# Separate buffers for the filter loop, two of chunk 0's matrix banks made earlier, and the filter banks read back in four steps

## Chip, cores and metric

The kernel runs on one core of a Trainium2 chip. The metric is the device time of one execution in microseconds (us), given as the median of several runs. Everything is float32. PE is the matrix engine, DVE the vector engine, ACT the scalar engine, POOL the GpSimd engine; SP is the engine that issues nearly all DMA transfers.

## The reference

The input is x of shape 8 x 1024 tokens x 128 channels (8 images of 32 x 32). Layer 0 adds an attention block to it. Layer 1 first adds a two-directional state-space block to the tokens t, and then adds a spectral filter of the layer-normed tokens. Only that last step matters here:

```
un  = layer_norm(t)                                  # per token
out = sum over k of  irfft(rfft(phi_k) * rfft(un)) @ (s_k * M_phi_plus[k])     # 16 filters
    + the same with un * (+1,-1,+1,...)  and M_phi_minus                       # signs undone after
    + un[t] @ M_u[0] + un[t-1] @ M_u[1] + un[t-2] @ M_u[2]                     # three-tap products
t   = t + out * (selected bank)                      # one of four filter banks, by log_weights + gumbel
```

The selected bank has 2 x 16 matrices of 128 x 128. For each of 128 frequencies the filters turn them into one matrix per frequency (a weighted sum over the 16 filters), and the spectra of the tokens are multiplied with it.

## The kernel before

All eight images stay on the chip through the first part, as tiles X[0] to X[7] of 128 partitions x 8 x 128. Then come three stages that matter here.

**End of the unit stage** (lines 1448 to 1545). The last two of 16 state-space units are finished while the layer norm, the spectra and the three-tap products of images 0 and 1 are already made. All engines, SP too, run in program order here. Near the end line 1541 adds the last unit's rows to X[7] and stores it to `xd`; line 1542 (`reload(u)`) reads it back in another order of tokens; line 1544 adds the three-tap products to X[1], and `store_residual(1)` (line 1545) writes X[1] to `xa`.

**Spectra stage** (lines 1558 to 1625, pools f_...). For images b = 2 to 7, `transform(b)` transposes the normed tokens on PE (cpt, line 561), multiplies them with the Fourier table (pf, line 571), combines the parts on ACT, DVE and POOL into sp, and stores sp (1 MB) to `ud`. One turn later `taps_of(b, k)` makes the three-tap products of two halves k (pu, line 601), adds them to X[b] on DVE (line 611), and `store_residual(b)` writes X[b] (512 KB) to `xa`. In between `turned(n, ...)` handles a quarter n of the selected bank's matrices: it loads 8 of them (`md`, 512 KB), transposes them on PE (mdt), copies them on DVE and stores them to `me` in DRAM. After the fourth quarter, four transfers read all of `me` back into `mst`, so that its partition is the filter number (32 of them) times the group g of four. PE, DVE, ACT and POOL run in program order; the order of SP is left to the scheduler.

**Filter loop** (lines 1629 to 1744, pools g_...). There are 16 chunks of 8 frequencies. `matrices(c, n, gs)` makes an eighth n of chunk c's frequency matrices: 16 products of mst and taps on PE (pg), into four PSUM banks, and four copies to gs, alternately by ACT and DVE. `loaded_spectra(c)` loads the chunk's spectra u from `ud` and makes their turned copy on POOL. `apply` multiplies them with gs (py). The loop runs one chunk ahead: chunk c + 1's matrices stand between the four applies of chunk c, and chunk 0's eight banks stand alone in front. gs (64 KB per partition) and u (8 KB) have two buffers each in pool g_2. These lie where the X tiles lay (`middle.close()`, lines 1626 and 1627, gives that space back), so the first gs waits for the last X to be stored. Then a last stage fetches the filtered spectra back (early_yt, room), transforms them (pz) and writes the output.

The lines that order the spectra stage, before:

```
for b in range(2, B + 1):
    ...
    if b > 2:
        taps_of(b - 1, 0)
    if 2 <= b <= 5:
        turned(b - 2, *((ps_o, "o", 4) if b == 2 else (ps_t, "t", 8)))
    if b > 2:
        taps_of(b - 1, 1)
        store_residual(b - 1)
```

The whole functions, with the profile's line numbers:

Of the kernel before, what the change touches and what calls it, by code (L numbers as in the profile page):

```python
# [10 lines left out]
ALU = mybir.AluOpType  # L11
# [34 lines left out]
def fast_kernel(ctx: ExitStack, tc: tile.TileContext, a: dict, out: bass.AP, bad: bass.AP):  # L46
# [883 lines left out]
    with ExitStack() as s:  # L930
# [608 lines left out]
        scale_rows(u)  # L1539
        third = shift_of(3, resid, *norms.pop(3), "_next")  # L1540
        add_rows(u)
        reload(u)
        for k in range(NB):
            add_taps(1, k, po[:, k])
        store_residual(1)
# [7 lines left out]
    with ExitStack() as s:  # L1553
        mp = s.enter_context(tc.tile_pool(name="c_m", bufs=1, side="right"))
        mst = mp.tile([P, 32, C], F32, tag="mst", name="mst")
        early_yt = mp.tile([P, 2, 4, 4, C], F32, name="early_yt")

        with ExitStack() as s2:
            p1 = s2.enter_context(tc.tile_pool(name="f_1", bufs=1))
            p2 = s2.enter_context(tc.tile_pool(name="f_2", bufs=2))  # L1560
            ps_f = s2.enter_context(tc.tile_pool(name="f_ps_f", bufs=2, space=PSUM))
            ps_o = s2.enter_context(tc.tile_pool(name="f_ps_o", bufs=2, space=PSUM))
            ps_t = s2.enter_context(tc.tile_pool(name="f_ps_t", bufs=1, space=PSUM))

            def turned(n, pool, tag, size):

                t = p2.tile([P, 8, C], F32, tag="md", name=f"md{n}")
                nc.sync.dma_start(t, md.rearrange("d r k e -> d (r k) e")[:, n * 8 : n * 8 + 8, :])
                to = p2.tile([P, 8, C], F32, tag="me", name=f"me{n}")
                for at in range(0, 8, size):  # L1570
                    pt = pool.tile([P, size, C], F32, tag=tag, name=f"mdt{n}_{at}")
                    for i in range(size):
                        nc.tensor.transpose(pt[:, i, :], t[:, at + i, :], ident)  # L1573
                    nc.vector.tensor_copy(
                        to[:, at : at + size].rearrange("p k d -> p (k d)"), pt.rearrange("p k d -> p (k d)")
                    )
                nc.sync.dma_start(me[:, n * 8 : n * 8 + 8, :], to)
                if n == 3:
                    for g in range(4):
                        nc.sync.dma_start(  # L1580
                            mst[g * 32 : (g + 1) * 32],
                            me[g * 32 : (g + 1) * 32].rearrange("n k d -> k n d"),
                        )

            def transform(b):

                un = xns.pop(b).rearrange("p (k r) c -> p k r c", k=NB)
                pt = ps_t.tile([P, NB, 4, P], F32, tag="t", name=f"cpt{b}")
                turn_spectra(un, pt)
                uts[b] = p2.tile([P, 4, NB * P + 1], F32, tag="ut", name=f"ut{b}")  # L1590
                nc.gpsimd.memset(uts[b][:, :, 0:1], 0.0)
                sp = p2.tile([P, NF // FC, NB, 2, 4, FC], F32, tag="sp", name=f"sp{b}")
                for k in range(NB):
                    pf = ps_f.tile([P, 4, 2, NF], F32, tag="f", name=f"pf{b}_{k}")
                    sd = p2.tile([P, 2, 2, 2, NF], F32, tag="sd", name=f"sd{b}_{k}")
                    later = p2.tile([P, 2, 2, NF], F32, tag="later", name=f"later{b}_{k}")
                    for _ in block_spectra(k, un, pf, sd, later, sp):
                        pass
                store_spectra(b, sp)
                copy_turned(uts[b], pt)  # L1600

            def taps_of(b, k):
                po = ps_o.tile([P, 4, C], F32, tag="o", name=f"pu{b}_{k}")
                regress(b, k, uts[b], po)
                add_taps(b, k, po)

            s2.enter_context(tc.manual_schedule(engines=IN_ORDER))
            uts = {}
            for _ in scaled(3, *third, p2):
                pass  # L1610
            for b in range(2, B + 1):
                if b + 2 < B:
                    norms[b + 2] = normalize(p2, b + 2)
                if b < B:
                    transform(b)
                if 3 < b + 1 < B:
                    for _ in normalized(b + 1, p2, *norms.pop(b + 1), wide=p2):
                        pass
                if b > 2:
                    taps_of(b - 1, 0)  # L1620
                if 2 <= b <= 5:
                    turned(b - 2, *((ps_o, "o", 4) if b == 2 else (ps_t, "t", 8)))
                if b > 2:
                    taps_of(b - 1, 1)
                    store_residual(b - 1)
        middle.close()
        middle.close()

        with ExitStack() as s2:
            p2 = s2.enter_context(tc.tile_pool(name="g_2", bufs=2))  # L1630
            p3 = s2.enter_context(tc.tile_pool(name="g_3", bufs=3))
            ps_g = s2.enter_context(tc.tile_pool(name="g_ps_g", bufs=8, space=PSUM))

            turn = 0

            def matrices(c, n, gs):

                nonlocal turn
                pts = [ps_g.tile([P, 4, P], F32, tag="g", name=f"pg{c}_{n}_{g}") for g in range(4)]
                cols = slice(c * FC, (c + 1) * FC)  # L1640
                for e in range(4):
                    for g in range(4):
                        rows = slice(g * 32, (g + 1) * 32)
                        nc.tensor.matmul(  # L1644
                            pts[g][:, e, :],
                            lhsT=mst[rows, n * 4 + e, :],
                            rhs=taps[rows, cols].rearrange("p f q m i -> p (f q m i)"),
                            start=True,
                            stop=True,
                        )  # L1650
                for g, pt in enumerate(pts):
                    to = gs[:, :, n * 16 + g * 4 : n * 16 + g * 4 + 4]
                    frm = pt.rearrange("p e n -> p n e")
                    if turn % 2:
                        nc.vector.tensor_copy(to, frm)  # L1655
                    else:
                        nc.scalar.copy(to, frm)  # L1657
                    turn += 1

            def loaded_spectra(c):  # L1660

                u = p2.tile([P, 2, NB, B, 2, 4 * FC], F32, tag="u", name=f"u{c}")
                for k in range(NB):
                    nc.sync.dma_start(
                        u[:, 0, k].rearrange("p b i f -> p b (i f)"), ud[c][:, :, k].rearrange("p b i q f -> p b (i q f)")
                    )
                nc.gpsimd.tensor_scalar(u[:, 1, :, :, 0, :], u[:, 0, :, :, 1, :], -1.0, None, ALU.mult)  # L1667
                nc.gpsimd.tensor_copy(u[:, 1, :, :, 1, :], u[:, 0, :, :, 0, :])
                return u

            def apply(c, n, q, gs, u, py):

# [42 lines left out]
                )  # L1715

            chunks = NF // FC
            gs, us, gathered = {}, {}, {}
            s2.enter_context(tc.manual_schedule(engines=IN_ORDER))
            for c in range(-1, chunks):  # L1720
                if c + 1 < chunks:
                    gs[c + 1] = p2.tile([P, P, C], F32, tag="gs", name=f"gs{c + 1}")
                    us[c + 1] = loaded_spectra(c + 1)
                else:

                    room = p2.tile([P, P, C], F32, tag="gs", name="room")
                    res = [room[:, :32, :], mp.tile([P, 32, C], F32, tag="mst", name="res1")]
                    res = [t.rearrange("p (b r) c -> p b r c", b=B) for t in res]
                    load_residuals(1, 0, B)
                    load_residuals(0, 0, 4)  # L1730

                for n in range(4):
                    if c + 1 < chunks:
                        matrices(c + 1, 2 * n, gs[c + 1])
                        matrices(c + 1, 2 * n + 1, gs[c + 1])
                    if c >= 0:
                        half, turn = divmod(n, 2)
                        py = ps_g.tile([P, 2, C], F32, tag="g", name=f"py{c}_{n}")
# [15 lines left out]
                if n == 2:  # L1754
                    load_residuals(0, 4, 4)
            for yt, (k, h) in zip(yts, pieces):
                z = p2.tile([P, 2, 2, 4, C], F32, tag="u", name=f"z{k}_{h}")
                for r, i, op in ((0, 0, ALU.subtract), (0, 1, ALU.add), (1, 0, ALU.add), (1, 1, ALU.subtract)):
                    nc.vector.tensor_tensor(z[:, r, i], yt[:, i, :, 2, :], yt[:, 1 - i, :, 3, :], op)
                blk = NB - 1 - k  # L1760
# [830 lines left out]
```

## Time and profile before

| what | value |
|---|---|
| median of 3 runs | 1403.44 us (1398.19 to 1407.6) |
| the profiled execution's own time | 1403.45 us |
| its span, first to last instruction | 1401.6 us |
| mean granted PE clock | 0.98 |
| busy share of the span | PE 95%, DVE 79%, ACT 66%, POOL 38% |

Busy times by stage, from windows of the trace (us):

| stretch | length | PE | DVE | ACT | POOL | PE clock | DMA share |
|---|---|---|---|---|---|---|---|
| 999 to 1010, image 2 and the first quarter of the bank | 11.0 | 5.7 | 5.4 | 4.0 | 7.9 | 0.87 | 0.96 |
| 1010 to 1022.4, image 3 | 12.4 | 12.4 | 7.4 | 5.3 | 8.0 | 0.84 | 0.65 |
| 1022.4 to 1033, image 4 | 10.6 | 10.6 | 7.8 | 5.3 | 7.4 | 1.00 | 0.76 |
| 1057.5 to 1069.2, last three-tap products | 11.7 | 10.9 | 4.8 | 1.6 | 6.1 | 1.00 | 1.18 |
| 1069.2 to 1076.4 | 7.2 | 2.1 | 0.5 | 0.6 | 0.0 | 0.93 | 0.61 |
| 1076.4 to 1088.4, chunk 0's matrices | 12.0 | 12.0 | 10.6 | 9.0 | 4.1 | 0.76 | 0.48 |
| 1105 to 1340, filter loop | 235.0 | 229.1 | 171.8 | 128.0 | 28.8 | 1.00 | 0.28 |

All times in this text are microseconds from the start of the span unless something else is said. A line of the profile names the source line, the engine and the tile that is written and those that are read (`gs<-pg`: the copy from PSUM tile pg to gs). A float32 product on PE shows as two records. A DMA issue on SP is shown with the time that issuing it took, not with the time of the transfer. The chain of waits is followed back from the last instruction: at each step to what released it. "Granted clock" is PE's clock as a share of full speed.

### The profile page before, as it was taken

Reading aid. Unit: us, or ns where it says so; the run is one execution under the profiler, and the core shown is the slowest. Engines: PE = TensorE matmul, PEld = TensorE weight load, DVE = VectorE, ACT = ScalarE, POOL = GpSimd, SP = SyncE. Lnnn points to the kernel's source line nnn. Section 1 sums busy time; section 2 is a strip of 40 time slices with the busy share of each in tenths; the row PEclk is TensorE's granted clock in tenths of the full one; section 3 lists DMA queues with packets and bytes.
Section 4 is the critical chain, followed back from the end, with each engine's and each line's share of the span. In section 5 each row is a group of like instructions: output and inputs, shape, how many; then the busy total and the mean of one; then the engine's idle time right before and its main releaser. Section 6 shows DMA issues by size and latency. Waiting matters only on the chain. (4 is left out here: it accounts for less than half of the span.)

```text
span 1401.6 us, 47569 instructions
## 1 busy us (share of the span) xinstructions
PE 1330.1 (95%) x20926; PEld 844.7 (60%) x20926; DVE 1103.4 (79%) x2145; ACT 922.8 (66%) x1428; POOL 536.0 (38%) x510
## 2 busy tenths in 40 slices
PE   7999999999999999999999999998898999999967
PEld 4333333333333666666666666667797988888964
DVE  5789888788778688988889898999564777777745
ACT  5666666766756888888878888876353555555520
POOL 3412986876910343434343343444673011111100
PEclk9999999999999999999999999999999999999979
DMA  7100111111101434444444343431668132222357
GB/s 172 55 2 2 38 39 39 53 39 39 31 1 42 96 78 93 108 94 113 94 108 94 92 95 88 114 83 48 197 208 198 46 78 73 77 69 70 83 171 294
DMA packets 139391, 123.24 MB, mean 88 GB/s; under 512 B 44808, under 2 KB 118152, under 8 KB 135080
## 3 DMA queue, kind: packets, MB, share of 16 engines
q1 hardware_dynamic: 137048, 115.93, 32.0%
q8 instruction: 166, 2.72, 0.8%
q10 hardware_dynamic: 2128, 4.19, 0.8%
q14 instruction: 49, 0.40, 0.1%
HBM read 78.15 MB, written 34.08 MB: 80 GB/s over the span
## 5 line engine op out<-in xcount | busy, mean ns | idle before, releaser
L809 ACT ACTIVATE pr<-pt 128x1024 f32<-128x1024 f32 x256 | 248.2, 1022 | 105.0 <-PE pt L804 103.9
L1657 ACT COPY gs<-pg 128x512 f32<-128x512 f32 x256 | 133.1, 603 | 75.6 <-PE pg L1644 58.4
L1655 DVE COPY gs<-pg 128x512 f32<-128x512 f32 x256 | 159.1, 685 | 26.0 <-PE pg L1644 18.9
L834 DVE TENSOR_TENSOR two<-pr,pr 128x1024 f32<-128x1024 f32 x128 | 164.8, 1328 | 15.2 <-ACT pr L809 15.2
L804 PE MATMUL pt<-q,k 32*128 32x512 f32 x1024 | 162.5, 651 | 6.1 <-ACT pr L809 4.1
L1644 PE MATMUL pg<-taps,mst 32*128 32x128 f32 x4096 | 150.1, 283 | 11.9 <-issue 5.8
L1644 PEld LDWEIGHTS pg<-taps,mst 32*128 32x128 f32 x4096 | 135.0, 189 | 27.2 <-issue 19.3
L825 PE MATMUL po<-pr,v 128*32 128x512 f32 x1024 | 140.6, 610 | 0.0
L1678 PE MATMUL py<-gs,u 128*32 128x128 f32 (+1 forms) x4096 | 130.9, 281 | 3.4 <-issue 3.4
L1030 POOL TENSOR_TENSOR ec<-ec,ct 128x2048 f32<-128x2048 f32 x16 | 83.6, 5224 | 112.3 <-ACT ct L1110 57.1
L1072 DVE SCALAR_TENSOR_TENSOR xs<-xp,cw,xs 128x1024 f32<-128x1024 f32 x96 | 122.5, 1283 | 2.2 <-issue 0.2
L1678 PEld LDWEIGHTS py<-gs,u 128*32 128x32 f32 (+1 forms) x4096 | 114.8, 141 | 10.9 <-issue 3.6
L1094 PE MATMUL pb<-bxt,wbc 128*128 128x512 f32 x256 | 114.0, 597 | 3.6 <-ACT zs L1085 3.6
L1667 POOL TENSOR_SCALAR u<-u 128x512 f32<-128x512 f32 x16 | 24.0, 1499 | 237.5 <-DMA u<-ud 138.3
L804 PEld LDWEIGHTS pt<-q,k 32*128 32x128 f32 x1024 | 49.5, 185 | 88.9 <-ACT pr L809 27.1
L1193 DVE SCALAR_TENSOR_TENSOR state<-state,dec,pst 128x64 f32<-128x64 f32 x448 | 87.3, 275 | 1.1
L1302 POOL TENSOR_TENSOR rms<-rms_v,mhalf 128x8 f32<-128x8 f32 x16 | 26.5, 1659 | 157.0 <-DVE rms_v L1300 157.0
L1094 PEld LDWEIGHTS pb<-bxt,wbc 128*128 128x128 f32 x256 | 47.1, 189 | 60.3 <-issue 55.0
L825 PEld LDWEIGHTS po<-pr,v 128*32 128x32 f32 x1024 | 27.8, 110 | 89.7 <-issue 86.4
L1016 POOL TENSOR_TENSOR lm<-cs,lm 128x2048 f32<-128x2048 f32 x16 | 57.9, 3620 | 57.7 <-DVE xs L1072 22.6
L845 PE MATMUL pd<-two,ones 128*32 128x512 f32 x512 | 74.1, 618 | 2.3 <-DVE two L834 2.1
L1272 PEld LDWEIGHTS spo<-wo,y 128*128 128x128 f32 x512 | 62.1, 191 | 13.1 <-issue 8.9
(310 smaller groups left out, 2784.5 us busy)
## 6 DMA issues: line engine op xcount, KB each, us to landing
lm<-cd SPq DMA_DIRECT2D x32, 512.0 KB
ec<-cd SPq DMA_DIRECT2D x32, 512.0 KB
ud<-sp SPq DMA_DIRECT2D x8, 1024.0 KB
u<-ud SPq DMA_DIRECT2D x32, 256.0 KB
yd<-sums SPq DMA_DIRECT2D x32, 256.0 KB
moved<-state SPq DMA_DIRECT2D x48, 128.0 KB
room<-yd SPq DMA_DIRECT2D x6, 1024.0 KB
X<-in_x SPq DMA_DIRECT2D x8, 512.0 KB
```

The costliest lines, as they stand in the source:

```text
L804: nc.tensor.matmul(pt[:, i, :], lhsT=k[rows, j * P : (j + 1) * P], rhs=q[rows, cols], start=True, stop=True)
L809: nc.scalar.activation(pr[:, 2 * g : 2 * g + 2, :].rearrange("p i t -> p (i t)"), pt.rearrange("p i t -> p (i t)"), AF.Exp, scale=SCALE,)
L825: nc.tensor.matmul(po[rows, :], lhsT=vs[b][:, j, rows], rhs=pr[:, h, :], start=(j == 0), stop=(j == NT - 1))
L834: nc.vector.tensor_tensor(two, sums["pr"][:, 2 * g : 2 * g + 2, :], pr[:, 2 * g : 2 * g + 2, :], ALU.add)
L1030: t = nc.gpsimd.tensor_tensor(u.ec, u.ec, u.ct.unsqueeze(1).to_broadcast([P, NH, NT, L]), ALU.mult)
L1072: u.convolved = nc.vector.scalar_tensor_tensor(acc, xp[:, at : at + T], cw[u.d][:, n, i : i + 1], acc, ALU.mult, ALU.add)
L1094: nc.tensor.matmul(u.pb[:, i * 512 : (i + 1) * 512], lhsT=wbc[u.d][:, k, :], rhs=xt[:, at : at + 512], start=(k == 0), stop=(k == KC - 1),)
L1193: nc.vector.scalar_tensor_tensor(u.state[:, k, h, :], u.state[:, k - 1, h, :], u.dec[:, c, h, j : j + 1], u.pst[c][:, j, h, :], ALU.mult, ...
L1644: nc.tensor.matmul(pts[g][:, e, :], lhsT=mst[rows, n * 4 + e, :], rhs=taps[rows, cols].rearrange("p f q m i -> p (f q m i)"), start=True, ...
L1655: nc.vector.tensor_copy(to, frm)
L1657: nc.scalar.copy(to, frm)
L1678: nc.tensor.matmul(py[t * 32 : t * 32 + 32 - 16 * m, q // 2, :], lhsT=u[:, i, m:, :, :, q * FC + f].rearrange("p k b i -> p (k b i)"), rhs ...
```

## The change

Three things are done.

1. **Buffers.** gs and u no longer rotate in one pool with two buffers. Even chunks take `first_gs`, a pool on the other side of the memory that is opened before the spectra stage and does not overlap X; odd chunks take `second_gs`, opened in the filter loop where X lay. early_yt moves to a pool of its own, opened in the filter loop. `room` and the z tiles of the last stage take the same two pools in turn.
2. **Two banks earlier.** `matrices` gets its PSUM tiles from its caller. `double_banks` makes a bank of chunk 0 in the spectra stage, with two of that stage's pf tiles. `planned` puts one after the first half of image 7's three-tap products and one after the second half. Chunk 0's spectra are loaded at the end of the spectra stage.
3. **Banks one by one.** Three quarters of the bank are loaded up front, the fourth when the first has been transposed. `turned(0)` to `turned(3)` stand at b = 3 to 6 instead of 2 to 5, all with the same PSUM tile. `spread(n)` reads quarter n back into mst at the beginning of turn b = n + 4, with four transfers of 8 partitions each (128 KB) in place of four of 32 partitions each (512 KB) at the end. The spectra stage now runs SP in program order too, and `reload` of X[7] stands there, behind the first bank load.

```diff
-        reload(u)
         for k in range(NB):
             add_taps(1, k, po[:, k])
         store_residual(1)
...
-        early_yt = mp.tile([P, 2, 4, 4, C], F32, name="early_yt")
+        first_gs = s.enter_context(tc.tile_pool(name="c_g", bufs=1, side="right"))
+
+        def chunk_matrices(c, pool):
+            return pool.tile([P, P, C], F32, tag="gs", name=f"gs{c}")
...
+            def load_bank(n):
+                mds[n] = pm.tile([P, 8, C], F32, tag="md", name=f"md{n}")
+                nc.sync.dma_start(mds[n], md.rearrange("d r k e -> d (r k) e")[:, n * 8 : n * 8 + 8, :])
+
+            def turned(n):
+
+                if n == 0:
+                    load_bank(3)
+                pt = ps_t.tile([P, 8, C], F32, tag="t", name=f"mdt{n}")
+                for i in range(8):
+                    nc.tensor.transpose(pt[:, i, :], mds[n][:, i, :], ident)
                 to = p2.tile([P, 8, C], F32, tag="me", name=f"me{n}")
...
+                nc.vector.tensor_copy(to.rearrange("p k d -> p (k d)"), pt.rearrange("p k d -> p (k d)"))
+                nc.sync.dma_start(me[:, n * 8 : n * 8 + 8, :], to)
+
+            def spread(n):
+                for g in range(4):
+                    nc.sync.dma_start(
+                        mst[g * 32 + n * 8 : g * 32 + n * 8 + 8],
+                        me[g * 32 : (g + 1) * 32, n * 8 : n * 8 + 8].rearrange("n k d -> k n d"),
                     )
-                nc.sync.dma_start(me[:, n * 8 : n * 8 + 8, :], to)
-                if n == 3:
-                    for g in range(4):
-                        nc.sync.dma_start(
-                            mst[g * 32 : (g + 1) * 32],
-                            me[g * 32 : (g + 1) * 32].rearrange("n k d -> k n d"),
-                        )
...
-            s2.enter_context(tc.manual_schedule(engines=IN_ORDER))
-            uts = {}
-            for _ in scaled(3, *third, p2):
+            s2.enter_context(tc.manual_schedule(engines=ALL_IN_ORDER))
+            uts, mds = {}, {}
+            for n in range(3):
+                load_bank(n)
+                if n == 0:
+                    reload(units[-1])
+            gs, begun = {0: chunk_matrices(0, first_gs)}, set()
+
+            def double_banks(n):
+                pts = [ps_f.tile([P, 2, 4, P], F32, tag="f", name=f"pg0_{n}_{i}") for i in range(2)]
+                begun.add((-1, n))
+                matrices(0, n, gs[0], [pts[g // 2][:, g % 2] for g in range(4)])
+
+            def ahead(b, place):
+                for _ in range(planned.get((b, place), 0)):
+                    double_banks(len(begun))
+
+            planned = {(B, 1): 1, (B, 2): 1}
+            for _ in scaled(3, *third, px):
                 pass
             for b in range(2, B + 1):
+                if 4 <= b <= 7:
+                    spread(b - 4)
...
+                ahead(b, 0)
                 if b > 2:
                     taps_of(b - 1, 0)
-                if 2 <= b <= 5:
-                    turned(b - 2, *((ps_o, "o", 4) if b == 2 else (ps_t, "t", 8)))
+                ahead(b, 1)
+                if 3 <= b <= 6:
+                    turned(b - 3)
                 if b > 2:
                     taps_of(b - 1, 1)
                     store_residual(b - 1)
+                ahead(b, 2)
+            us = {0: loaded_spectra(0, first_gs)}
...
+            second_gs = s2.enter_context(tc.tile_pool(name="g_g", bufs=1))
+            yp = s2.enter_context(tc.tile_pool(name="g_y", bufs=1, side="right"))
+            early_yt = yp.tile([P, 2, 4, 4, C], F32, name="early_yt")
...
                 if c + 1 < chunks:
-                    gs[c + 1] = p2.tile([P, P, C], F32, tag="gs", name=f"gs{c + 1}")
-                    us[c + 1] = loaded_spectra(c + 1)
+                    if c >= 0:
+                        gs[c + 1] = chunk_matrices(c + 1, second_gs if c % 2 == 0 else first_gs)
+                        us[c + 1] = loaded_spectra(c + 1, second_gs if c % 2 == 0 else first_gs)
...
-                        matrices(c + 1, 2 * n, gs[c + 1])
-                        matrices(c + 1, 2 * n + 1, gs[c + 1])
+                        for i in range(2 * n, 2 * n + 2):
+                            if (c, i) not in begun:
+                                matrices(c + 1, i, gs[c + 1], single_banks(c + 1, i))
...
-                z = p2.tile([P, 2, 2, 4, C], F32, tag="u", name=f"z{k}_{h}")
+                z = (second_gs if h else first_gs).tile([P, 2, 2, 4, C], F32, tag="u", name=f"z{k}_{h}")
```

More of the change, by code (lines that the diff above doesn't have):

```diff
@@ L1555, in fast_kernel, with loaded_spectra, matrices @@
         mst = mp.tile([P, 32, C], F32, tag="mst", name="mst")
-        early_yt = mp.tile([P, 2, 4, 4, C], F32, name="early_yt")
+        first_gs = s.enter_context(tc.tile_pool(name="c_g", bufs=1, side="right"))
+        def chunk_matrices(c, pool):
+            return pool.tile([P, P, C], F32, tag="gs", name=f"gs{c}")
+        def loaded_spectra(c, pool):
+            u = pool.tile([P, 2, NB, B, 2, 4 * FC], F32, tag="u", name=f"u{c}")
+            for k in range(NB):
+                nc.sync.dma_start(
+                    u[:, 0, k].rearrange("p b i f -> p b (i f)"), ud[c][:, :, k].rearrange("p b i q f -> p b (i q f)")
+                )
+            nc.gpsimd.tensor_scalar(u[:, 1, :, :, 0, :], u[:, 0, :, :, 1, :], -1.0, None, ALU.mult)
+            nc.gpsimd.tensor_copy(u[:, 1, :, :, 1, :], u[:, 0, :, :, 0, :])
+            return u
+        turn = 0
+        def matrices(c, n, gs, pts):
+            nonlocal turn
+            cols = slice(c * FC, (c + 1) * FC)
+            for e in range(4):
+                for g in range(4):
+                    rows = slice(g * 32, (g + 1) * 32)
+                    nc.tensor.matmul(
+                        pts[g][:, e, :],
+                        lhsT=mst[rows, n * 4 + e, :],
+                        rhs=taps[rows, cols].rearrange("p f q m i -> p (f q m i)"),
+                        start=True,
+                        stop=True,
+                    )
+            for g, pt in enumerate(pts):
+                to = gs[:, :, n * 16 + g * 4 : n * 16 + g * 4 + 4]
+                frm = pt.rearrange("p e n -> p n e")
+                if turn % 2:
+                    nc.vector.tensor_copy(to, frm)
+                else:
+                    nc.scalar.copy(to, frm)
+                turn += 1
         with ExitStack() as s2:
-            p1 = s2.enter_context(tc.tile_pool(name="f_1", bufs=1))
+            px = s2.enter_context(tc.tile_pool(name="f_x", bufs=2))
             p2 = s2.enter_context(tc.tile_pool(name="f_2", bufs=2))
+            pm = s2.enter_context(tc.tile_pool(name="f_m", bufs=3))
             ps_f = s2.enter_context(tc.tile_pool(name="f_ps_f", bufs=2, space=PSUM))
@@ L1563, in fast_kernel @@
             ps_t = s2.enter_context(tc.tile_pool(name="f_ps_t", bufs=1, space=PSUM))
-            def turned(n, pool, tag, size):
-                t = p2.tile([P, 8, C], F32, tag="md", name=f"md{n}")
-                nc.sync.dma_start(t, md.rearrange("d r k e -> d (r k) e")[:, n * 8 : n * 8 + 8, :])
-                to = p2.tile([P, 8, C], F32, tag="me", name=f"me{n}")
[L1570 to L1575, printed above, removed]
-                    )
-                nc.sync.dma_start(me[:, n * 8 : n * 8 + 8, :], to)
-                if n == 3:
-                    for g in range(4):
-                        nc.sync.dma_start(
-                            mst[g * 32 : (g + 1) * 32],
-                            me[g * 32 : (g + 1) * 32].rearrange("n k d -> k n d"),
-                        )
+            def load_bank(n):
[7 more added lines that the diff above has]
+                    nc.tensor.transpose(pt[:, i, :], mds[n][:, i, :], ident)
+                to = p2.tile([P, 8, C], F32, tag="me", name=f"me{n}")
+                nc.vector.tensor_copy(to.rearrange("p k d -> p (k d)"), pt.rearrange("p k d -> p (k d)"))
+                nc.sync.dma_start(me[:, n * 8 : n * 8 + 8, :], to)
+            def spread(n):
+                for g in range(4):
+                    nc.sync.dma_start(
+                        mst[g * 32 + n * 8 : g * 32 + n * 8 + 8],
+                        me[g * 32 : (g + 1) * 32, n * 8 : n * 8 + 8].rearrange("n k d -> k n d"),
+                    )
             def transform(b):
@@ L1616, in fast_kernel @@
                 if 3 < b + 1 < B:
-                    for _ in normalized(b + 1, p2, *norms.pop(b + 1), wide=p2):
+                    for _ in normalized(b + 1, p2, *norms.pop(b + 1), wide=px):
                         pass
+                ahead(b, 0)
                 if b > 2:
                     taps_of(b - 1, 0)
-                if 2 <= b <= 5:
-                    turned(b - 2, *((ps_o, "o", 4) if b == 2 else (ps_t, "t", 8)))
+                ahead(b, 1)
+                if 3 <= b <= 6:
+                    turned(b - 3)
                 if b > 2:
@@ L1631, in fast_kernel, with single_banks @@
             p3 = s2.enter_context(tc.tile_pool(name="g_3", bufs=3))
+            second_gs = s2.enter_context(tc.tile_pool(name="g_g", bufs=1))
+            yp = s2.enter_context(tc.tile_pool(name="g_y", bufs=1, side="right"))
+            early_yt = yp.tile([P, 2, 4, 4, C], F32, name="early_yt")
             ps_g = s2.enter_context(tc.tile_pool(name="g_ps_g", bufs=8, space=PSUM))
[L1634 to L1669, printed above, removed]
+            def single_banks(c, n):
+                return [ps_g.tile([P, 4, P], F32, tag="g", name=f"pg{c}_{n}_{g}") for g in range(4)]
             def apply(c, n, q, gs, u, py):
@@ L1717, in fast_kernel @@
             chunks = NF // FC
-            gs, us, gathered = {}, {}, {}
+            gathered = {}
             s2.enter_context(tc.manual_schedule(engines=IN_ORDER))
@@ L1721, in fast_kernel @@
                 if c + 1 < chunks:
-                    gs[c + 1] = p2.tile([P, P, C], F32, tag="gs", name=f"gs{c + 1}")
-                    us[c + 1] = loaded_spectra(c + 1)
+                    if c >= 0:
+                        gs[c + 1] = chunk_matrices(c + 1, second_gs if c % 2 == 0 else first_gs)
+                        us[c + 1] = loaded_spectra(c + 1, second_gs if c % 2 == 0 else first_gs)
                 else:
-                    room = p2.tile([P, P, C], F32, tag="gs", name="room")
+                    room = chunk_matrices(c + 1, first_gs)
                     res = [room[:, :32, :], mp.tile([P, 32, C], F32, tag="mst", name="res1")]
```

## The prediction

> **What bounds the kernel now.** I read the page first (PE busy 95% of the span), then the chain of waits through the two stages that the change touches, then SP's and DVE's orders of time there, then windows for the DMA rates. The profiled execution took 1403.45 us of device time with a span of 1401.6; the median of the runs shown is 1403.44, so a difference in the span is taken over to the median as it is. One run in three strayed by 5 us.
>
> The chain of waits (start, us, what):
>
> ```profile
> 999.19 1.75 PE pf L571 x8
> 1000.95 6.92 DMA md<-md
> 1008.00 1.94 PE mdt L1573 x8
> 1009.94 1.71 PE cpt L561 x8
> 1011.65 4.65 PE pf L571 x16
> ...
> 1057.66 10.73 PE pu L601 x96
> 1068.42 0.76 DVE X L611
> ...
> 1069.60 5.75 DMA xa<-X
> ...
> 1076.45 12.06 PE pg L1644 x250
> ```
>
> PE carries the chain except for two holes. In the first, PE waits 5.11 us for a bank (md<-md), and then works slowly: mdt 1.94 for what later takes 0.87, cpt 1.71 for 0.87, pf 4.65 for 3.46. In the second, chunk 0's first copies wait until the last residual store has left X, because gs lies where X lay; PE idles 5.16 us, and the prologue then lasts to the first apply at 1088.43. From there PE is full to 1346, and nothing in the change touches that loop's work.
>
> DVE ends the prologue: 12 of its copies of 128x512 follow each other without a gap, 0.61 each, beside PE's 1.05 per bank (2.1 for two):
>
> ```profile
> 1082.42 7.27 DVE L1655 COPY gs<-pg 128x512 f32<-128x512 f32 x12 [0.42 <-PE pg L1644]
> ```
>
> SP's order of time near the read-back of the banks, and DMA windows (last two columns: mean busy share of the DMA engines, GB/s; the column before them is PE's clock):
>
> ```profile
> 1044.13 0.37 SPq L592 DMA_DIRECT2D ud<-sp  x1
> 1044.61 1.81 SPq L1577 DMA_DIRECT2D me<-me  x1
> 1046.85 0.85 SPq L614 DMA_DIRECT2D xa<-X  x1
> 1050.90 4.57 SPq L1580 DMA_DIRECT2D mst<-me  x4
> 1058.40 6.37 SPq L614 DMA_DIRECT2D xa<-X  x1
> ```
>
> ```profile
> 661.00:669.00 8.00, 8.00 (x57) 5.37 (x57) 6.51 (x7) 5.83 (x7) 0.00 (x0) 1.00 1.03 216
> 1008.00:1009.00 1.00, 1.00 (x5) 1.00 (x6) 0.00 (x0) 0.00 (x0) 1.00 (x3) 0.50 1.00 287
> 1048.50:1051.00 2.50, 2.50 (x25) 2.50 (x24) 1.67 (x4) 1.95 (x6) 2.50 (x7) 1.00 1.04 398
> 1054.00:1063.00 9.00, 9.00 (x68) 8.59 (x67) 3.45 (x6) 2.15 (x4) 5.53 (x11) 1.00 1.23 180
> ```
>
> Stores from 128 partitions (me, xa) run at 398 GB/s. The loads lm and ec, into 64 partitions each, run at 216 with the engines full. The read-back mst<-me, into 32 partitions per transfer, runs at 180. Its 2 MB held the rings from 1052 to 1063[...].
>
> [...] The fetches into early_yt (8 partitions) write 8 completions each in the trace. [...]
>
> **The change part by part.**
>
> First hole: turned(0) goes from b=2 to b=3, and banks 0 to 2 are asked for ahead. On SP, in program order now, md0 follows xa(1) at about 1001.3 and lands near 1009; PE wants it at 1011.6. PE passes from pf (ends 1002.88) to cpt3, which waits only for ACT's copies of cpt2 (end 1004.49). A hole of 1.7 us should leave the clock up. cpt3 0.87 + pf 3.46 from 1004.55 gives 1008.9 instead of 1016.29: **-7.4**. mdt3 now falls into b=6, +0.87; pu(7,0) ends at 1059.2.
>
> Banks ahead: two of the eight banks (1.05 each on PE) stand around pu(7,1). Their four ACT copies fall in ACT's idle 16.49 us; of the four on DVE two fit DVE's gap of 1.93 between add_taps, and two start the prologue. Nothing is added on PE, only moved.
>
> Buffers apart: gs0 no longer waits for xa. If the banks were there in time: pu(7,0) 1059.2 + 1.05 + pu(7,1) 2.68 + 1.05 + 0.1 + 16 DVE copies at 0.615 (18 before, two done) 9.84 = first apply at 1073.9 against 1088.43, **-14.5**. u0 would come 6 us after xa(7), and POOL's 1.51 + 0.60 fit. Chunk 1's copies now wait for xa(7), some 10 us after it was issued: covered. early_yt's new place, the z tiles' pools and the reload issued behind md0 cost nothing: the fetches begin at 1108, z keeps its rotation, X7 is wanted at b=5, over 10 us later. If that cover were gone, each would cost its landing, about 6.
>
> Read-back one by one: four transfers of 512 KB become sixteen of 128 KB, 12 more issues on SP (four took 4.57). Each goes to 8 partitions. Four follow one another per bank set[...]. Call T the time that they hold those rings. [...] From below: the fetch at 1177.9 moved its 128 KB by 1179.4, 85 GB/s, so 6.2; [...]a 512 B packet at the 27 ns of the ud store, 128 per engine, 3.5. The fetch is short[...] (169 GB/s at first, 26 at its end), so I take T = **9.5**.
>
> SP is in order here. Per b it holds: read-back of the bank before (waits for that me to land), ud (1 MB), me, xa. From ud's issue to me landed is 6.77 (1044.13 to 1050.90), so one turn takes 6.75 + T, against PE's 10.56 (0.87 + 3.46 + 2.68 + 0.87 + 2.68). With T = 9.5 it is 16.3: the rings fall behind by 5.7 a turn. The first read-back starts about 1027.3 (ud3 waits for POOL until 1017.5; + 6.77 + 1.6 for md3 + 1.05 issue and rounding 0.4). The fourth has landed at 1027.3 + 3 x 6.75 + 4T + 1 = 1048.6 + 4T = **1086.6**. Every bank's matmuls read all 128 partitions of mst, so pg0 stands until then from 1059.2, and behind it in PE's order pu(7,1), behind that add_taps, xa(7) and u0. After 27 us PE is at half clock for about 6 us: pg0 2.1, pu(7,1) 4.65, pg1 1.05, then 0.1 + 9.84: 17.7. First apply at 1104.3 against 1088.43: **+15.9**. sp6 and sp7 would wait up to 6 us for late ud stores, beside PE. Sum: 1403.4 + 15.9 = 1419.3.
>
> **The rivals.**
> Read-back harmless (the other side): the four small transfers hide beside the products. One mechanism decides, T, in the 8-partition read-back: 1066.3 + 4T = 1088.4 gives T = 5.5. Below it the change wins: T = 3.5 lands at 1062.6 and gives 1066.3 + 4 x 3.5 = 1080.3, -8, 1395; from T = 2.6 down the whole -14.5 stays, 1389. For it: the fetch's first 64 KB ran at full packet speed (84 ns for 2 KB). Against: its last packets took 300 ns and more[...].
> A draw: T between 5 and 6, the front's gain paid back by the stall, 1401 to 1406. For it stands the 85 GB/s[...].
> The change doing less than it says: if SP still put the bank loads late, PE would keep the first hole; the rest stays as above, and with T = 9.5 the rings' start moves little: 1419 to 1426.
>
> **How the numbers follow.** A change of 1%, 14 us, is about what a measurement of this kernel can tell from none. Read-back bound, with the late-load case: 0.78; T from 6.2 to 11.7 gives +2.7 to +24.7, own range 1406 to 1428. Harmless: 0.17, 1389 to 1399. Draw: 0.05. Slower by over 1% needs T above 9.0, about two thirds of the first case: 0.52. Faster by over 1% needs nearly the whole -14.5: 0.06. Within 1%: 0.42. The range leaves out the best of the harmless case and the worst of the first: 1395 to 1428.
>
> **What would show it.** Right: PE goes from pf to cpt3 without a bank wait, clock 1.00 at 1008; the four mst<-me of each b lie 16 us apart on SP; PE's longest wait is pg on mst, over 20 us; 0.50 after it. Wrong: the last mst<-me issued before 1056 and pg0 near 1060; or DMA rates over 100 GB/s in those stretches.

## The result, and the profile after

Measured side by side, the kernel before took 1401.54 us (median of 6 runs) and the changed one 1415.72 (6 runs, 1409.88 to 1422.45): ratio 1.0104, interval 1.0066 to 1.0143. The change made the kernel about 1% slower. The profiled execution of the changed kernel took 1414.91 us, with a span of 1413.2.

The chain of waits of this execution names only its last two steps, so PE's order of time is read instead (start, busy time, what; in brackets the idle time before it and what ended it):

```profile
1004.73 1.09 PE L561 MATMUL cpt<-ident,ln_x 128*128 128x128 f32 x8 [1.66 <-ACT ut L566]
1005.65 3.62 PE L571 MATMUL pf<-fwd,ln_x 128*128 128x256 f32 x16
...
1051.35 8.20 PE L601 MATMUL pu<-m_u,ut 128*128 128x128 f32 x72
1078.64 0.79 PE L1580 MATMUL pg<-taps,mst 32*128 32x128 f32 x2 [19.09 <-DMA mst<-me]
1081.30 0.79 PE L1580 MATMUL pg<-taps,mst 32*128 32x128 f32 x2 [1.87 <-DMA mst<-me]
1083.83 0.79 PE L1580 MATMUL pg<-taps,mst 32*128 32x128 f32 x2 [1.74 <-DMA mst<-me]
1086.03 2.07 PE L1580 MATMUL pg<-taps,mst 32*128 32x128 f32 x26 [1.41 <-DMA mst<-me]
1088.03 3.63 PE L601 MATMUL pu<-m_u,ut 128*128 128x128 f32 x24
1091.59 1.17 PE L1580 MATMUL pg<-taps,mst 32*128 32x128 f32 x32
1094.76 9.71 PE L1580 MATMUL pg<-taps,mst 32*128 32x128 f32 x256 [1.99 <-DVE gs L1591]
1104.40 2.02 PE L1710 MATMUL py<-gs,u 128*32 128x128 f32 x64
```

The first hole is gone: cpt waits 1.66 us for ACT, not 5.11 for a bank. From 1059.5 PE stands before the first early bank. Its four groups of partitions start one by one, about 2.5 us apart, each as its transfer lands, and the 19.09 is only the first of four waits. Behind it stand the last three-tap product and all else. The first apply comes at 1104.40, before at 1088.43.

SP's order of time in the changed kernel shows why mst is late (the number after the start is the time that issuing took):

```profile
1026.83 1.49 SPq L1621 DMA_DIRECT2D mst<-me  x4
1028.42 0.39 SPq L592 DMA_DIRECT2D ud<-sp  x1
1028.91 9.46 SPq L1617 DMA_DIRECT2D me<-me  x1
1038.42 0.42 SPq L614 DMA_DIRECT2D xa<-X  x1
1042.58 1.71 SPq L1621 DMA_DIRECT2D mst<-me  x4
...
1058.44 1.49 SPq L1621 DMA_DIRECT2D mst<-me  x4
...
1074.12 1.49 SPq L1621 DMA_DIRECT2D mst<-me  x4
```

The read-backs start 15.75, 15.86 and 15.68 us apart, where a turn on PE takes 10.56. The store to me, issued right behind one, needs 9.46 us just to be issued, though DVE had filled its tile by 1024.7; the first one, at 1020.24 with no read-back ahead of it, needed 1.25. What holds the issue itself, the trace doesn't show.

Windows (PE, PEld, DVE, ACT and POOL busy, then PE's clock, the DMA engines' mean busy share, GB/s):

```profile
1008.00:1009.00 1.00, 1.00 (x6) 0.87 (x6) 0.69 (x2) 0.21 (x1) 1.00 (x4) 1.00 1.00 395
1028.00:1038.00 10.00, 10.00 (x80) 9.64 (x79) 6.63 (x19) 5.34 (x12) 8.03 (x16) 1.00 0.83 113
1066.00:1076.00 10.00, 0.00 (x0) 0.00 (x0) 0.00 (x0) 0.00 (x0) 0.00 (x0) 0.50 0.69 181
```

At 1008 the clock is 1.00 where it was 0.50. From 1028 to 1038 the DMA engines are 83% busy and move only 113 GB/s, and that is read-back and a store to ud together; from 1034 to 1036, and again from 1081 to 1085, the read-back moves nearly alone, at 49 GB/s. From 1066 to 1076 no engine computes anything.

Executions start this stage up to 5 us apart. So the stretch from the start of image 2's pf products (999.19 before, 999.38 after) to the first apply is the measure used below: 89.24 us before, 105.02 after, **+15.8**. The span grew by 11.6 only, because the rest, from the first apply to the end, took 308.8 us against 313.2. Near the end PE is below full clock for a while in both: 0.74 from 1340.9 to 1363.9 in the kernel before, 0.92 from 1356 to 1376 in the changed one. Over the twelve kernels of this study this rest took from 305.1 to 313.2 us in the profiled execution; what sets it wasn't tried. The medians of many runs differ by 14.2 us, nearer to the stretch.

### The profile page after: what moved, and what is told of

Its sections match the earlier page's. It is cut to its first block, busy times and chain, and to the rows that moved or that the text cites. A ratio compares the mean times of both kernels' runs of the same rounds, so it can differ in the third digit from the quotient of the medians.

```text
span 1413.2 us, 47581 instructions
## 1 busy us (share of the span) xinstructions
PE 1326.1 (94%) x20926; PEld 840.2 (59%) x20926; DVE 1103.3 (78%) x2144; ACT 922.3 (65%) x1428; POOL 536.1 (38%) x510
## 5 line engine op out<-in xcount | busy, mean ns | idle before, releaser
L1580 PE MATMUL pg<-taps,mst 32*128 32x128 f32 x4096 | 151.4, 281 | 30.3 <-DMA mst<-me 24.1
```

The costliest lines, as they stand in the source:

```text
L1580: nc.tensor.matmul(pts[g][:, e, :], lhsT=mst[rows, n * 4 + e, :], rhs=taps[rows, cols].rearrange("p f q m i -> p (f q m i)"), start=True, ...
```

## The experiments

The theory, an estimate of the author's: the read-back is slow because the eight partitions of each transfer lie close together; it holds up the stores that SP issues behind it, so the turns of SP fall behind PE's, and an early bank puts its wait ahead of everything on PE. The rivals: the number of transfers, or SP's program order, makes it late; or the early banks alone cost the time. The kernel before took 1395.5 to 1395.7 us beside them, less than the 1401.5 beside the changed kernel, so where an expectation gives a total time, the ratio is what can be compared. "Stretch" is that from image 2's pf to the first apply, in one profiled execution of each kernel. The ratio is that of the runs taken side by side; it can differ a little from the quotient of the two medians.

| kernel | median, us | ratio to before | interval | stretch, us |
|---|---|---|---|---|
| before | 1395.5 to 1395.7 | 1 | | 89.2 |
| changed | 1415.72 (before: 1401.54) | 1.0104 | 1.0066 to 1.0143 | 105.0 |
| one read-back | 1397.69 | 1.0011 | 0.9985 to 1.0036 | 88.0 |
| every second partition | 1397.65 | 1.0012 | 0.9997 to 1.0028 | 89.7 |
| every fourth partition | 1393.72 | 0.9981 | 0.9960 to 1.0001 | 85.7 |
| no early banks | 1408.33 | 1.0093 | 1.0064 to 1.0121 | 99.8 |
| SP left to the scheduler | 1414.91 | 1.0127 | 1.0076 to 1.0178 | 105.4 |
| read-back right behind the stores, adjoining | 1401.34 | 1.0060 | 1.0036 to 1.0085 | 95.2 |
| the same, every fourth | 1385.45 | 0.9937 | 0.9913 to 0.9961 | 76.9 |
| the same, every fourth, no early banks | 1382.83 | 0.9932 | 0.9905 to 0.9958 | 76.2 |
| every fourth, no early banks | 1384.49 | 0.9926 | 0.9904 to 0.9949 | 78.7 |
| before, with the buffers alone | 1389.88 | 0.9966 | 0.9947 to 0.9985 | 81.7 |

In all ten experiments the ratio shows 0.2 to 3.6 us less gain, or more loss, than the stretch; why was not tried. So small differences between kernels whose intervals overlap rest on the stretch alone.

**One read-back.** The changed kernel with the old read-back: four transfers of 32 partitions, at b = 7.

```diff
+                if n < 3:
+                    return
-                        mst[g * 32 + n * 8 : g * 32 + n * 8 + 8],
-                        me[g * 32 : (g + 1) * 32, n * 8 : n * 8 + 8].rearrange("n k d -> k n d"),
+                        mst[g * 32 : (g + 1) * 32],
+                        me[g * 32 : (g + 1) * 32].rearrange("n k d -> k n d"),
```

> Undoes one part: the bank is read back once, after the fourth quarter, with four transfers of 32 partitions (512 KB each), at the place where the fourth quarter stood. Theory (few partitions, so the rings are held some 9 us by each quarter): held once for about 11.3 us; me of the fourth quarter lands near 1053.4, the last of mst near 1066.7, first apply near 1085 instead of 1104.4; time about 1397, 19 less than the changed kernel and 5 less than the one before. Rival 1 (SP's program order costs it, not the transfers): the order is kept, so 1410 or more. Rival 2 (the two banks in front of image 7's last products cost it): they stay, so about 1414.

PE's order of time:

```profile
1058.41 0.48 PE L1580 MATMUL pg<-taps,mst 32*128 32x128 f32 x2 [0.48 <-DMA mst<-me]
1061.20 0.67 PE L1580 MATMUL pg<-taps,mst 32*128 32x128 f32 x2 [2.31 <-DMA mst<-me]
1064.21 0.79 PE L1580 MATMUL pg<-taps,mst 32*128 32x128 f32 x2 [2.34 <-DMA mst<-me]
1066.75 2.07 PE L1580 MATMUL pg<-taps,mst 32*128 32x128 f32 x26 [1.76 <-DMA mst<-me]
```

The groups come 2.8 us apart here too, but each is now 512 KB (188 GB/s) instead of 128. The first apply is at 1085.78 where some 1085 was expected; but this execution began the stretch 1.6 us earlier than the changed kernel's, so that it came 2.4 us late. The ratio, 1.0011, is above the expected one (1397 against 1401.5 is 0.997). So the sixteen small transfers account for the loss, 17 us of stretch, but the early banks and buffers with the old read-back win next to nothing: pg0 still stands 8 us before its last group.

**Every fourth partition.** The same sixteen transfers, bytes and order; only the eight partitions of each now lie four apart, and the bank's quarters are loaded to match.

```diff
-                nc.sync.dma_start(mds[n], md.rearrange("d r k e -> d (r k) e")[:, n * 8 : n * 8 + 8, :])
+                nc.sync.dma_start(mds[n], md.rearrange("d r k e -> d (r k) e")[:, n::4, :])
-                        mst[g * 32 + n * 8 : g * 32 + n * 8 + 8],
+                        mst[g * 32 + n : g * 32 + 32 : 4],
```

> The same sixteen transfers of 8 partitions and 128 KB at the same places[...], but quarter n holds every fourth matrix, so its partitions are n, n+4, ... of each group of 32 rather than 8 adjoining ones. Theory[...]: a quarter takes about 3.5 us instead of 9.1, a turn about 10.3, less than PE's 10.56; mst is there by 1060, first apply near 1074; time about 1388. Rival 1 (SP's order) and a third one ([...]the number of transfers): nothing changes, 1415.

PE's order of time:

```profile
1063.45 0.48 PE L1580 MATMUL pg<-taps,mst 32*128 32x128 f32 x2 [2.55 <-DMA mst<-me]
1064.58 0.48 PE L1580 MATMUL pg<-taps,mst 32*128 32x128 f32 x2 [0.64 <-DMA mst<-me]
1065.43 0.48 PE L1580 MATMUL pg<-taps,mst 32*128 32x128 f32 x2 [0.38 <-DMA mst<-me]
1066.75 2.07 PE L1580 MATMUL pg<-taps,mst 32*128 32x128 f32 x26 [0.83 <-DMA mst<-me]
1068.75 4.98 PE L601 MATMUL pu<-m_u,ut 128*128 128x128 f32 x24
```

SP's order of time:

```profile
1039.11 3.14 SPq L1621 DMA_DIRECT2D mst<-me  x4
...
1042.86 3.37 SPq L1617 DMA_DIRECT2D me<-me  x1
...
1049.71 2.81 SPq L1621 DMA_DIRECT2D mst<-me  x4
```

The groups land 1.1 us apart, the read-backs start 10.8 us apart on SP, and the store behind one is issued in 3.3 to 3.8 us. So it is the partitions, 19.3 us of stretch from two slices, as the theory says; the bank loads, now gathered from every fourth matrix, hold PE up nowhere. But mst was expected by 1060 and the first apply near 1074, and they came at 1066.75 and 1086.47: the first read-back starts at 1028, and three turns of 10.8 and one landing later it is past 1066. A quarter of some 4 us (3.5 expected) wasn't enough to bring the whole gain; pg0 still waits, and pu behind it runs slowly (4.98, at a granted clock of 0.66 from 1066 to 1076, for what takes 2.95 where nothing waits, further down).

**Every second partition**, eight over sixteen.

```diff
-                        mst[g * 32 + n * 8 : g * 32 + n * 8 + 8],
+                        mst[g * 32 + n // 2 * 16 + n % 2 : g * 32 + n // 2 * 16 + 16 : 2],
```

> The changed kernel with each read-back of 8 partitions laid 2 apart, over 16 partitions; engines, bytes, issues and order as before. Theory[...]: T is half of the 9.1 us that 8 adjoining ones took, 4.6, or no longer than 5.5; turn on SP 11.3 to 12.3; last quarter landed near 1068 to 1072, first apply 88 to 92 us after the start of pf of b=2 (105.0 in the changed kernel, 85.7 with every fourth partition). Rival (it is being adjoining or not, or every fourth alone helps): the turn stays near 15.8 and the first apply at 103 to 106.

PE's order of time in this kernel:

```profile
1066.13 0.79 PE L1580 MATMUL pg<-taps,mst 32*128 32x128 f32 x2 [6.12 <-DMA mst<-me]
1067.58 0.79 PE L1580 MATMUL pg<-taps,mst 32*128 32x128 f32 x2 [0.66 <-DMA mst<-me]
1068.93 0.79 PE L1580 MATMUL pg<-taps,mst 32*128 32x128 f32 x2 [0.56 <-DMA mst<-me]
1070.23 2.07 PE L1580 MATMUL pg<-taps,mst 32*128 32x128 f32 x26 [0.52 <-DMA mst<-me]
```

The groups lie 1.37 us apart, the read-backs 11.8; the stretch is 89.7, as the theory had it. Eight partitions cost 2.46 us adjoining, 1.37 two apart, 1.10 four apart: it isn't a matter of adjoining or not, but of how far apart they lie. For the 131,072 B of a transfer that is 53, 96 and 119 GB/s: the first doubling of the distance is worth 1.8 times the rate, the second only 1.24 times.

With the rate, the time of one 512 B packet changes. Where little but the read-back moves, share and rate of a slice of the DMA view give it (an estimate: share x 16 engines x 512 B / rate; the share is known to a tenth). In the changed kernel, from 1034.00 to 1035.75, 0.6 to 0.7 and 49 GB/s give 100 to 117 ns; with every second partition, from 1053.25 to 1055.00, 0.5 to 0.6 and 100 GB/s give 41 to 49; with every fourth, from 1062.00 to 1063.75, 0.4 to 0.5 and 143 GB/s give 23 to 29, near the 27 ns that the prediction names for the ud store. No run varied the packets or the number of engines, and why the distance counts wasn't shown.

**No early banks**, and **SP left to the scheduler** in the spectra stage, each the changed kernel with one line changed:

```diff
-            planned = {(B, 1): 1, (B, 2): 1}
+            planned = {}
```

> The changed kernel without the two banks in the spectra stage (all eight in the filter loop's front). Theory: mst still lands at 1086, image 7's last products are no longer held behind it, then all eight banks; 18 copies of DVE and the gaps of the cold clock, 12.5: first apply near 1099; time about 1411, 4 less than the changed kernel. Rival 2 (the early banks cost it): 1391 to 1400.

```diff
-            s2.enter_context(tc.manual_schedule(engines=ALL_IN_ORDER))
+            s2.enter_context(tc.manual_schedule(engines=IN_ORDER))
```

> The changed kernel with SP's order in the spectra stage left to the scheduler, as it was before the change. Theory: the rings still get 15.3 us of work per turn of 10.56 (ud 3.4, me 1.4, xa 1.4, read-back 9.1), so mst lands within 8 us of 1086; time 1407 to 1421. Rival 1 (SP's program order): mst lands near 1060 to 1066; 1388 to 1397.

Without early banks the last group starts at 1085.20 and the first apply follows 13.06 us later; in the changed kernel it follows 18.37 later. The early banks cost 5.2 us of stretch when mst is late (5.4 expected for the first apply): without them pu(7,1) runs inside the wait. The ratios of the two kernels, 1.0093 and 1.0104, don't tell them apart. PE's order of time without them:

```profile
1050.43 10.88 PE L601 MATMUL pu<-m_u,ut 128*128 128x128 f32 x96
1077.83 0.76 PE L1580 MATMUL pg<-taps,mst 32*128 32x128 f32 x2 [16.51 <-DMA mst<-me]
```

All 96 records of pu stand in front of the wait here. SP's order of time with SP left to the scheduler:

```profile
1043.40 3.71 SPq L1621 DMA_DIRECT2D mst<-me  x4
...
1059.15 3.31 SPq L1621 DMA_DIRECT2D mst<-me  x4
...
1073.67 3.32 SPq L1621 DMA_DIRECT2D mst<-me  x4
```

The read-backs lie 15.5, 15.8 and 14.5 us apart and the stretch is 105.4, that of the changed kernel: holding SP to program order isn't the cause. Another place in that order does help, as the next runs show.

**The place of the read-back.** The quarter is read back in the turn that stores it, right behind the stores of me and ud and ahead of xa. For that the store to ud moves too, from ahead of the store to me to behind it; the two moves weren't run apart.

```diff
-                store_spectra(b, sp)
+                if 3 <= b <= 6:
+                    held[b] = sp
+                else:
+                    store_spectra(b, sp)
...
-                if 4 <= b <= 7:
-                    spread(b - 4)
...
                 if 3 <= b <= 6:
                     turned(b - 3)
+                    store_spectra(b, held.pop(b))
+                    spread(b - 3)
```

With every fourth partition, and then with adjoining ones:

> Every-fourth-partition read-back as in the run before it (turn 10.8 us), and on SP the read-back of quarter b-3 is issued right after store_spectra(b)'s two stores, ahead of the xa fetches, so the last quarter's read-back stands right behind ud of b=6. Theory ([...]its place in the queue sets when it begins): the last quarter lands near 1059 on the changed kernel's time scale, as pg0 falls due at 1059; the stall on mst is 0 to 1.5 us and the clock holds; first apply 1074 to 1076, some 12 to 13 us less than before: ratio near 0.991. Rival (the read-back is late for another reason than its place): mst still lands after 1063, ratio 0.998 as with every fourth partition alone.

> The changed kernel's adjoining partitions, with the read-back of quarter b-3 issued right after b's two stores. Theory (length and place both count, and the length holds the rings): the turn stays 15.5 to 16 us, the last quarter begins one turn earlier by count of b but behind three long ones, lands near 1079 on the changed kernel's scale, first apply 95 to 99 us after the start of pf of b=2, ratio near 1.005. Rival (the place alone was what mattered in the run with both): first apply 77 to 80, ratio 0.994.

PE's order of time, every fourth partition:

```profile
1050.62 8.20 PE L601 MATMUL pu<-m_u,ut 128*128 128x128 f32 x72
1058.75 1.18 PE L1580 MATMUL pg<-taps,mst 32*128 32x128 f32 x32
1059.85 2.95 PE L601 MATMUL pu<-m_u,ut 128*128 128x128 f32 x24
1062.73 1.17 PE L1580 MATMUL pg<-taps,mst 32*128 32x128 f32 x32
1065.89 9.71 PE L1580 MATMUL pg<-taps,mst 32*128 32x128 f32 x256 [1.99 <-DVE gs L1591]
1075.53 2.01 PE L1713 MATMUL py<-gs,u 128*32 128x128 f32 x64
```

No wait for mst is left, and the first apply comes at 1075.53; the stretch is 12.4 us less than before, as expected (12 to 13). The ratio, 0.9937, is a little above the expected 0.991. PE's order of time with adjoining partitions:

```profile
1073.26 2.07 PE L1580 MATMUL pg<-taps,mst 32*128 32x128 f32 x26 [0.47 <-DMA mst<-me]
...
1091.66 2.01 PE L1713 MATMUL py<-gs,u 128*32 128x128 f32 x64
```

Here the stretch is 95.2 and the ratio 1.0060, both as expected; its turns, 14.2, 15.3 and 14.0, are somewhat shorter than the 15.5 to 16 named. The stores to me are issued there in under 0.5 us, but SP waits four times, 33.3 us in all, for them to land before it may read them back: what is queued behind the slow transfers comes late either way. The four kernels make a square: the partitions are worth 19.3 us (105.0 to 85.7) at the old place and 18.3 (95.2 to 76.9) at the new one; the place is worth 9.8 and 8.8. They add up.

**Early banks, when mst is nearly or quite in time.** `planned = {}` in the two kernels with every fourth partition.

> Every-fourth-partition read-back, no early banks: pu of b=7 is no longer behind pg0. Theory (an early bank that waits on mst costs its wait to the whole of PE's queue): mst lands near 1066.8 and the first apply comes 13.1 us after that, as in the run of the changed kernel without early banks, 1079.8 against 1086.5 with them: ratio near 0.993. Rival (the early banks are worth their time also when a little late): first apply 1087 or later, ratio 0.998 or more.

> As the run with the read-back right behind the stores, but no early banks: all eight banks after pu of b=7. Theory: mst is there in time, so here the early banks do gain: this one is 1.5 to 2.5 us behind the one with them, first apply 1075.5 to 1078, ratio near 0.993. Rival (early banks only cost): this one is faster than the one with them by 2 us or more.

At the old place the stretch falls from 85.7 to 78.7, 7.0 us, as expected (6.7). At the new place it falls by 0.65 us; a loss of 1.5 to 2.5 was expected, and the rival's 2 us gain didn't come either. PE's order of time at the new place without early banks:

```profile
1049.18 10.88 PE L601 MATMUL pu<-m_u,ut 128*128 128x128 f32 x96
1060.91 12.62 PE L1580 MATMUL pg<-taps,mst 32*128 32x128 f32 x320 [0.85 <-DVE X L611]
1073.45 2.01 PE L1713 MATMUL py<-gs,u 128*32 128x128 f32 x64
```

From the end of pu to the first apply it is 13.4 us here and 12.7 with early banks; those put off the end of pu(7,1) by 1.3, with the bank ahead of it. The gap of 1.99 in front of the last 256 (0.85 here) eats much of what they save: with early banks the first product in the filter loop's own PSUM pool waits for DVE's copies to gs, without them for DVE's last add to X. Early banks gain nothing in this kernel.

**The buffers alone**, in the kernel before: gs and u in the two new pools, everything else as it was.

```diff
+        first_gs = s.enter_context(tc.tile_pool(name="c_g", bufs=1, side="right"))
...
+            us = {0: loaded_spectra(0, first_gs)}
...
+            second_gs = s2.enter_context(tc.tile_pool(name="g_g", bufs=1))
```

> The kernel before with its filter-loop buffers alone laid apart; one read-back, no early banks, queue order as before. Theory: the 7.4 us hole at the first prime factor product goes, pu of b=7 ends near 1068.4, the first copies of the tap banks near 1070.3 in place of 1075.8, 18 VectorE copies then take 11.07 us: first apply near 1081.5 against 1088.4, ratio 0.995. Rival (the hole was not in the buffers, or the b=7 chain is bound by the stores and fetches instead of PE): first apply stays within 1.5 us of 1088.4, ratio 1.000.

The expectation mixes up the holes: the 7.4 us and the place (its "prime factor product" is pf) are the first hole's, and its numbers are the second's, the one before chunk 0's first copies. PE's order of time with the buffers alone:

```profile
1007.75 1.94 PE L1613 MATMUL mdt<-ident,md 128*128 128x128 f32 x8 [5.05 <-DMA md<-md]
...
1068.67 12.15 PE L1581 MATMUL pg<-taps,mst 32*128 32x128 f32 x320 [0.84 <-DVE X L611]
1080.75 2.01 PE L1703 MATMUL py<-gs,u 128*32 128x128 f32 x64
```

PE still waits 5.05 us for the first bank, with mdt at 1.94. The second hole has gone: the first pg follow pu without the wait of 5.16, and the first apply is at 1080.75 (expected 1081.5), stretch 7.5 us shorter; the ratio, 0.9966, is worth 4.7 us (interval 2.1 to 7.4). The two holes are separate; the bank order removes one, the buffers the other.

The fastest kernels here are those with every fourth partition and no early banks; 0.9926 and 0.9932 can't be told apart. Both beat the kernel before by about 10 us.

## Why the prediction was right

It gave 1419.3, 15.9 us over the kernel before; measured were 1415.72, 14.2 over. The rival that the read-back is harmless fell, as did the draw and the one that the first hole stays. That the change would be slower by over 1% it held for as likely as not (0.52); the measured 1.04% lies on that line, with an interval on both sides.

- **First hole, -7.4.** Right. pf ends near 1009.1 where 1008.9 was forecast, the wait for ACT is 1.66 (1.7), and the clock stays at 1.00, which had been an estimate.
- **T, 9.5 us.** Right within half a microsecond, from two sides: the turn of 15.76 less 6.75 gives 9.0, four landings 2.46 apart give 9.8. That the rate would fall so far was the author's estimate: the only transfer to 8 partitions that the prediction measured was a short fetch. The 3.5 rests on 128 packets per engine, an estimate from the 8 completions of each such fetch and the 27 ns of the ud store. The 6.2 from a single fetch was too short, as suspected; why was not tried. The runs with the partitions two and four apart show that their distance sets the time (2.46, 1.37 and 1.10 us for 128 KB), not by what mechanism.
- **Turns and landing.** The fourth read-back was issued at 1074.12 where the sum had 1076.0 (1027.3 + 3 x 16.25), and took 11.9 us to its last group where it had 10.5. Two errors, opposite; the last group started at 1086.03, forecast 1086.6. So the forecast of the start came out closer than its parts, by luck. The early bank didn't stand until then as one piece: it ran group by group, which changed nothing.
- **From landing to first apply, 17.7.** 18.37 measured, with two terms off. pu(7,1) took 3.63, not 4.65: the clock was back at 1.00 by 1090, 4 us after the last group began, where 6 were forecast from the kernel before (0.50 there from 1077 to 1082). The pause after the second early bank was put at 0.1 and took 1.99 for the PSUM tiles. Again the two partly cancel. The same term made the prediction's best case, the 14.5 us without a stall, too large: 12.4 came in the kernel that has no stall, and 13.0 in the one without early banks.
- **Sum, +15.9 on the first apply.** +15.97, on the stretch +15.8. The span moved by 11.6 and the medians by 14.2; the prediction took it that nothing past the first apply differs, and the profiled executions scatter there by up to 8 us.
- **Signs.** PE went from pf to cpt without a bank wait, the clock was 1.00 at 1008, the read-backs lay 15.8 us apart, and the clock was 0.50 after the wait, as forecast. The longest single wait on mst was 19.09, under the 20 named; the four together make 24.1. One sign of being wrong came as well, over 100 GB/s (113 from 1028 to 1038), but a store to ud runs in that stretch, and the read-back alone moved 49.
- **A shorter T.** The sum 1066.3 + 4T gives a win of 4.5 to 6 us for the T of every fourth partition (4.4 by its landings, 4.1 by its turn); it won 3.5 of stretch. That another place for the read-back would be worth 8.8 more, the prediction didn't consider.

## What to carry to other kernels

See how far apart the partitions of a transfer lie before cutting it into pieces: here eight adjoining partitions were 2.2 times slower than the same bytes to every fourth partition (2.46 us for 128 KB, against 1.10), and the store behind the slow read-back took 9.46 us to issue, against 3.3 to 3.8. Work moved ahead on an in-order engine takes its wait along (5.2 us of stretch in the changed kernel): put it where its input is surely there, or behind what would otherwise fill the wait. And where a change has parts, run each alone: here, in stretch, the buffers alone were worth 7.5 us, and buffers and bank order 13.0 once the read-back was in time; all of it was lost in a read-back that came 28 us dearer than the same transfers with other partitions and another place.

## What the runs showed of the hardware

The bandwidth of a read-back in rows of 512 B went by how far apart its eight partitions lie: 53, 96 and 119 GB/s for partitions one, two and four apart. Placing them needed nothing but strided slices, at the read-back and at the bank loads. The second doubling of the distance gave little, 119 against 96; by the estimate above a packet took 100 to 117 ns with adjoining partitions and 23 to 29 with every fourth.
